# The last batches of a two-layer residual-norm kernel: residual rows added by TensorE, two batches' rows kept in PSUM, openings ahead of closings

## The chip, the cores and the metric

The kernel runs on one core of a Trainium2 chip. The metric is the device time in microseconds of one execution, as the median of several runs. A core has TensorE (PE in the profile: matmuls), VectorE (DVE), ScalarE (ACT), GpSimd (POOL) and SyncE (SP, which here issues the DMAs). SBUF is the working memory. PSUM is where TensorE writes[...].

## The reference

The input x has 128 batches of 128 rows by 512 columns. Layer 0 adds a per-row maximum and normalises. Layer 1 is multi-head attention, a projection, a normalisation inside, a residual sum and a normalisation outside:

```
# layer 0, adj is 128 x 128, b has 128 values
A   = einsum('od,bdn->bon', adj, x);  C = A + b[None, :, None]
x   = layernorm(x + max over the last axis of relu(A[:, :, None, :] + (C - A)[:, :, :, None]))
# layer 1, 8 heads, the mask is adj
q, k, v = split(x @ w_qkv)
o   = softmax(where(adj == 0, -inf, q k^T / sqrt(64))) v
o   = o @ w_proj + b_proj
ln  = (o - mean(o)) * rsqrt(var(o) + 1e-5) * ln_gamma + ln_beta
out = layernorm(x + o + ln)
```

In the kernel's terms, for one batch: r is the row of x after layer 0 (with ln_beta added to it beforehand), o the projected row, and z = (o - mean) * rs * gamma + (o + r), where rs = (var + 1e-5)^-0.5. The output is z normalised again.

## The kernel before

All arithmetic is in float32. Batches are worked on in groups of four (G = 4, NG = 32 groups), and in pairs inside a group. The projections of four batches are a Unit: a 2 x 2 block product by seven half-size products, whose partial sums live in four PSUM banks (b1 to b4) and which `result`, `relay` and `relayed` put together and write to SBUF. The order on every engine is the order in which the program is written (`pin` keeps it): no planner is at work. Where engines depend on one another, semaphores are inserted.

A main loop handles the pairs in a staggered way, and behind it an end section is written out by hand. With L = 127, the end section names the batches L - 7 = 120 to L = 127 one by one. What matters for the change is how the tail, from o to the output, is done for them:

- Batches 116, 117, 122 and 123 go the way of GpSimd: ScalarE normalises o into z (`tail_inner_one`), GpSimd does three residual steps on z (`tail_residual_one`: times gamma, plus o, plus r), ScalarE takes the statistics of z (`scalar_stats`: two accumulating passes per batch, whose unneeded output goes to a PSUM tile "trash"), GpSimd finishes them (`finish_scalar_stats`: names de, me), and ScalarE normalises and stores (`tail_outer_one`).
- Batches 120, 121 and 124 to 127 go the fused way on VectorE: statistics of o (`bn`: BATCH_NORM_STATS2 and BATCH_NORM_AGGREGATE, names st and mv), an **opening** (`fused_open`: z = (o - mean) * gamma, one scalar_tensor_tensor, L624, and r = o + r, a tensor_tensor that shows as L77), a **closing** (`fused_close`: z = z * rs + r, L632), and statistics of z. `finish_stats` has GpSimd work out rs by an addition and a power, and for those columns that ScalarE will normalise with, a shift (VectorE times -1, L267, then GpSimd). The last batch, 127, is normalised by VectorE itself (`tail_outer_vector`, L653).
- Batches 120 and 121 come out of the Unit of group 30 as `os_[30, 0]`, an SBUF tile. Batches 124 to 127 are projected directly: `last_seed` puts the bias in a PSUM bank, and `last_project` adds four products of 128 x 512 to it (names pp). Their rows o are read in PSUM.

The residual rows r of 118 to 121 wait in the SBUF tile "early", those of 122 to 127 in spare room of the tile "wlast", whose other part holds the projection's weights. The tile names zl and z in the profile are the z rows; pss0 and pss1 are the two PSUM banks that the attention scores used.

Three engines' queues matter in the end section. TensorE's order is: projection of 124, attention of 126 and 127, projections of 125, 126 and 127. VectorE's order is that of the openings, closings and statistics as written. GpSimd does residual steps, scales and finishes in the written order. SP issues the stores in the order of the `tail_outer` calls.

Of the kernel before, what the change touches and what calls it, by code (L numbers as in the profile page):

```python
# [9 lines left out]
F32 = mybir.dt.float32  # L10
AF = mybir.ActivationFunctionType
ALU = mybir.AluOpType
# [4 lines left out]
def kernel(  # L17
# [30 lines left out]
    nc = tc.nc  # L48
    B, P, D = x.shape
# [3 lines left out]
    G = 4  # L53
    GT = G * P
    HT = GT // 2
    HE = D // 2
    NG = B // G
# [11 lines left out]
    psum = ctx.enter_context(tc.tile_pool(name="psum", bufs=1, space=bass.MemoryType.PSUM))  # L69

    pin = tc.keep_in_program_order

    def pe(*args, **kwargs):
        pin(nc.tensor.matmul(*args, **kwargs))  # L74

    def tt(eng, dst, a, b, op):
        pin(eng.tensor_tensor(dst, a, b, op))  # L77
# [69 lines left out]
    ident = const.tile([P, P], F32, name="ident")  # L147
# [14 lines left out]
    class Unit:  # L162
# [28 lines left out]
            pin(nc.scalar.copy(self.new_bank(2), self.banks[1]))  # L191

        def relayed(self):
            pin(nc.scalar.copy(self.out[0, 0], self.banks[2]))

        def result(self, half, col):
            bank, k = {(0, 0): (2, 1), (0, 1): (3, 2), (1, 0): (4, 3), (1, 1): (3, 3)}[half, col]
            pin(
                nc.vector.tensor_tensor(  # L199
                    self.out[half, col], self.banks[bank], self.snaps[k], ALU.add  # L200
                )
            )

    def left_sums(name, a11, a12, a21, a22):
        s = [
            sb.tile([P, 2, HT], F32, tag=f"{name[0]}s{k}", name=f"s{k}_{name}") for k in range(1, 5)
        ]
        return dict(zip((1, 2, 3, 4, 5, 6, 7), (a11, a12, s[3], a22, s[0], s[1], s[2]))), (
            (s[0], a21, a22, ALU.add),
            (s[1], s[0], a11, ALU.subtract),  # L210
            (s[2], a11, a21, ALU.subtract),
            (s[3], a12, s[1], ALU.subtract),
        )
# [20 lines left out]
    def tokens_stationary(w):  # L234
        def mm(bank, i, left, first):
            for k in range(2):
                for c in range(2):
                    pe(
                        bank[:, k],
                        lhsT=left[:, c, ts(k, P)],  # L240
                        rhs=w[:, i, c],
                        start=first and k == 0 and c == 0,
                        stop=True,
                        skip_group_check=True,
                    )

        return mm
# [28 lines left out]
    def normalize(dst, src, key):  # L276
        rs, sh = stat_of.pop(key)
        pin(nc.scalar.activation(dst, src, AF.Identity, bias=sh, scale=rs))  # L278
# [104 lines left out]
    pss, prob, psums, pT, pos, oT = {}, {}, {}, {}, {}, {}  # L383
    nmax = {}

    def place(b):
        g, j = divmod(b, G)
        return g, j // 2, j % 2
# [109 lines left out]
    o_lefts, os_ = {}, {}  # L498
# [5 lines left out]

    def o_unit(g):
        for h in range(2):
            tag, bufs = ("x", 2) if (g, h) == (NG - 2, 0) else ("o", 3)
            os_[g, h] = sb.tile([P, 2, D], F32, tag=tag, name=f"o_{g}_{h}", bufs=bufs)
        out = {(h, c): os_[g, h][:, :, ds(c * HE, HE)] for h in range(2) for c in range(2)}
        return Unit(f"o_{g}", o_lefts.get(g), tokens_stationary(wp), out)  # L510


# [19 lines left out]
    def last_project(b, w):  # L532
        g, h, jj = place(b)
        for c in range(KC):
            pe(
                os_[b],
                lhsT=oT[g, h][:, c, ts(jj, P)],
                rhs=w[:, c],
                start=False,
                stop=True,  # L540
                skip_group_check=True,
            )
# [4 lines left out]
    def o_of(b):  # L547
        g, h, jj = place(b)
        return os_[b] if b in os_ else os_[g, h][:, jj]
# [19 lines left out]
    rs_, zp = {}, {}  # L569
# [31 lines left out]
    def z_tile(b):  # L601
        q, j = divmod(b, 2)
        tag, bufs = {58: ("xt", 2), 59: ("xt", 2), 60: ("z", 1), 61: ("qk0", 2)}.get(q, ("xs", 1))
        if tag == "xs":
            zs[b] = sb.tile([P, D], F32, tag=f"xs{b - B + G + 1}", name=f"z_{b}")
            return
        if q not in ends:
            ends[q] = sb.tile([P, 2, D], F32, tag=tag, name=f"zl_{q}", bufs=bufs)
        zs[b] = ends[q][:, j]
# [5 lines left out]
    def tail_residual_one(b, steps=range(3)):  # L615
        for k in steps:
            with_, op = ((ga_bc, ALU.mult), (o_of(b), ALU.add), (rs_[b], ALU.add))[k]
            tt(nc.gpsimd, zs[b], zs[b], with_, op)

    def fused_open(b, mean):  # L620

        z_tile(b)
        pin(
            nc.vector.scalar_tensor_tensor(  # L624
                zs[b], o_of(b), mean, ga_bc, ALU.subtract, ALU.mult
            )
        )
        tt(nc.vector, rs_[b], o_of(b), rs_[b], ALU.add)

    def fused_close(b):  # L630
        z, (rs, _) = zs[b], stat_of.pop(("o", b))
        pin(nc.vector.scalar_tensor_tensor(z, z, rs, rs_[b], ALU.mult, ALU.add))  # L632

    def tail_outer_one(b):
        z = zs.pop(b)
        normalize(z, z, ("z", b))
        pin(nc.sync.dma_start(out=out[b], in_=z))
# [8 lines left out]
    def stats(name, *items, fused=0):  # L646
        stat = columns(name, *items)
        finish_stats(*stat, fused)
        return stat[0]
# [6 lines left out]
    def scalar_stats(*batches):  # L656

        n, name = len(batches), f"{batches[0]}"
        trash = psum.tile([P, D], F32, tag="pss0", name=f"trash_{name}")
        sums, mean, dev = (  # L660
            small.tile([P, NC], F32, tag=f"{t}1", name=f"{t}1_{name}") for t in ("su", "me", "de")
        )
        act = nc.scalar.activation
        for k, b in enumerate(batches):
            pin(act(trash, zs[b], AF.Identity, accum_out=sums[:, k : k + 1]))
        pin(act(mean[:, :n], sums[:, :n], AF.Identity, scale=-1.0 / D))
        for k, b in enumerate(batches):
            pin(
                act(
                    trash, zs[b], AF.Square, bias=mean[:, k : k + 1], accum_out=dev[:, k : k + 1]  # L670
                )
            )
        return batches, mean, dev

    def finish_scalar_stats(stat):
        batches, sh, rs = stat
        n = len(batches)
        pin(nc.gpsimd.tensor_scalar(rs[:, :n], rs[:, :n], 1.0 / D, EPS, ALU.mult, ALU.add))
        tt(nc.gpsimd, rs[:, :n], rs[:, :n], mhalf.to_broadcast([P, n]), ALU.pow)
        tt(nc.gpsimd, sh[:, :n], sh[:, :n], rs[:, :n], ALU.mult)  # L680
        for k, b in enumerate(batches):
            stat_of["z", b] = rs[:, k : k + 1], sh[:, k : k + 1]
# [98 lines left out]
    for p in range(LAST):  # L781
        g, ph = divmod(p, 2)
        a, b = 2 * p, 2 * p + 1
        first = v_unit(0) if p == 0 else qk_unit(g + 1, ph)
        n = p + 4 if p + 4 < B // 2 else None
        f = p + 5 if p + 5 < B // 2 else None
        ta, tb, to = tails(p)
        mv = small.tile([P, NC, 2], F32, tag="mv", name=f"mv_{p}")
# [152 lines left out]
    L = B - 1  # L941
# [10 lines left out]
    mv = small.tile([P, NC, 2], F32, tag="mv", name=f"mv_{LAST}")  # L952
# [101 lines left out]
    wlast, room = last_load()  # L1054
# [101 lines left out]
    mv = stats("last_5", ("o", L - 7), ("o", L - 6), fused=2)  # L1156
    attend_copy(L - 1)
    attend_copy(L)
    last_project(L - 1, wlast)
    last_project(L, wlast)  # L1160
    stat = scalar_stats(L - 11, L - 10)
    tail_residual_one(L - 5, [0])
    fused_open(L - 7, mv[:, 0, 0:1])
    mv1 = stats("last_6", ("o", L - 3), fused=1)
    tail_residual_one(L - 5, [1, 2])
    fused_open(L - 3, mv1[:, 0, 0:1])
    fused_close(L - 7)
    fused_close(L - 3)
    finish_scalar_stats(stat)
    for t in (L - 11, L - 10):  # L1170
        tail_outer_one(t)
    stat5 = scalar_stats(L - 5)
    fused_open(L - 6, mv[:, 1, 0:1])
    mv = stats("last_7", ("o", L - 2), ("z", L - 3), ("z", L - 7), fused=1)
    fused_open(L - 2, mv[:, 0, 0:1])
    fused_close(L - 6)
    fused_close(L - 2)
    tail_residual_one(L - 4)
    for t in (L - 7, L - 3):
        tail_outer_one(t)  # L1180
    mv = stats("last_8", ("o", L - 1), ("z", L - 2), ("z", L - 6), fused=1)
    fused_open(L - 1, mv[:, 0, 0:1])
    fused_close(L - 1)
    finish_scalar_stats(stat5)
    stat4 = scalar_stats(L - 4)
    for t in (L - 6, L - 2, L - 5):
        tail_outer_one(t)
    finish_scalar_stats(stat4)
    mv = stats("last_9", ("o", L), ("z", L - 1), fused=1)
    fused_open(L, mv[:, 0, 0:1])  # L1190
    for t in (L - 4, L - 1):
        tail_outer_one(t)
    fused_close(L)
    mv = stats("last_10", ("z", L), fused=1)
    tail_outer_vector(L, mv[:, 0, 0:1])


# [39 lines left out]
```

## Time and profile before

| | |
|---|---|
| median of 3 runs | 1956.71 us (1956.1 to 1957.49) |
| profiled execution | 1958.7 us, its span 1957.0 us |
| PE, DVE, ACT, POOL busy | 1933.8, 1563.4, 1065.1, 1294.9 us |
| chain that ended last | PE 94%, DVE 2%, POOL 2%, ACT 1%, DMA 1% |
| last matmul ends | 1940.64 us into the span |
| last VectorE instruction | 1953.36 to 1953.91 us |
| last store issued | 1953.93 us |

The difference between the profiled execution and its span lies outside the span, in what surrounds it. In a timeline, each line gives the start in us, the duration in us, the engine, the line of the program, the operation, output <- inputs by tile name, shapes and count, and in brackets the idle time ahead of the instruction with what ended it. In a table of windows each pair is an engine's busy time in the window and, in brackets, its number of instructions, then TensorE's granted clock, the DMA share and the GB/s moved. A chain that ended last is followed back from the last instruction.

### The profile page before, as it was taken

Reading aid. Unit: us, or ns where it says so; the run is one execution under the profiler, and the core shown is the slowest. Engines: PE = TensorE matmul, PEld = TensorE weight load, DVE = VectorE, ACT = ScalarE, POOL = GpSimd, SP = SyncE. Lnnn points to the kernel's source line nnn. Section 1 sums busy time; section 2 is a strip of 40 time slices with the busy share of each in tenths; the row PEclk is TensorE's granted clock in tenths of the full one; section 3 lists DMA queues with packets and bytes.
Section 4 is the critical chain, followed back from the end, with each engine's and each line's share of the span. In section 5 each row is a group of like instructions: output and inputs, shape, how many; then the busy total and the mean of one; then the engine's idle time right before and its main releaser. Section 6 shows DMA issues by size and latency. Waiting matters only on the chain.

```text
span 1957.0 us, 33035 instructions
## 1 busy us (share of the span) xinstructions
PE 1933.8 (99%) x11533; PEld 1637.0 (84%) x11533; DVE 1563.4 (80%) x2516; ACT 1065.1 (54%) x3094; POOL 1294.9 (66%) x820
## 2 busy tenths in 40 slices
PE   8999999999999999999999999999999999999996
PEld 6888888888888888888888888888888888888884
DVE  6767778778788787787787877877878878778787
ACT  3444555545546555555465565554554655555565
POOL 6336666767667676667676676766767766767647
PEclk9999999999999999999999999999999999999998
DMA  6657576575675665766756757667667667576564
GB/s 217 161 136 179 145 194 164 167 207 153 172 193 157 189 173 166 201 154 172 204 153 180 188 157 194 170 165 196 162 171 194 160 186 177 161 201 164 148 216 140
DMA packets 444934, 341.74 MB, mean 175 GB/s; under 512 B 276832, under 2 KB 378336, under 8 KB 444768
## 3 DMA queue, kind: packets, MB, share of 16 engines
q1 hardware_dynamic: 444336, 338.85, 63.8%
q8 instruction: 91, 1.49, 0.3%
q10 hardware_dynamic: 432, 0.79, 0.1%
q14 instruction: 75, 0.61, 0.1%
HBM read 172.82 MB, written 166.72 MB: 174 GB/s over the span
## 4 chain that ended last, share of the span: by engine, by line
PE 94%; DVE 2%; POOL 2%; ACT 1%; DMA 1%; issue 0%; SPq 0%; POOLq 0%; ACTq 0%; DVEq 0%
PE b_qk L74 39%; PE b_v L74 19%; PE b_o L74 18%; PE pss L74 6%; PE po L74 6%; PE pa L74 5%; POOL zl L77 1%; DVE st_mv_last L255 0%; ACT s L424 0%; POOL s_o L77 0%; DMA x<-in_x_dram 0%; DMA pT<-hop 0%; POOL rs_mv_last L77 0%; DMA hop<-pu 0%; DVE amax L291 0%
## 5 line engine op out<-in xcount | busy, mean ns | idle before, releaser
L74 PE MATMUL b_qk<-s_x,wqk 128*128 128x256 f32 x2048 | 473.6, 379 | 1.0 <-DVE qk L199 0.8
L74 PEld LDWEIGHTS b_qk<-s_x,wqk 128*128 128x128 f32 x2048 | 388.8, 190 | 55.4 <-DVE qk L199 1.5
L424 ACT ACTIVATE s<-s,nmax 128x128 f32<-128x128 f32 x1024 | 396.2, 392 | 5.3 <-DVE nmax L417 5.3
L74 PE MATMUL b_qk<-x1T,wqk 128*128 128x256 f32 x1536 | 360.1, 384 | 0.1
L74 PEld LDWEIGHTS b_qk<-x1T,wqk 128*128 128x128 f32 x1536 | 287.8, 191 | 45.5 <-issue 1.0
L77 POOL TENSOR_TENSOR z<-z,ga_bc 128x1024 f32<-128x1024 f32 x58 | 164.6, 2838 | 167.1 <-ACT z L278 167.1
L269 POOL TENSOR_SCALAR rs_mv<-mv 128x6 f32<-128x6 f32 (+2 forms) x61 | 14.7, 241 | 386.3 <-DVE mv L256 386.3
L77 DVE TENSOR_TENSOR s<-s,rec 128x1024 f32<-128x1024 f32 x128 | 252.8, 1975 | 4.4
L186 ACT COPY u_qk<-b_qk 128x512 f32<-128x512 f32 x192 | 112.5, 586 | 243.3 <-PE b_qk L74 242.4
L74 PE MATMUL b_v<-wv,s_x 128*128 128x256 f32 x1024 | 237.1, 379 | 0.0
L74 PE MATMUL b_o<-wp,s_o 128*128 128x256 f32 x992 | 229.6, 379 | 0.2 <-ACT u_o L186 0.2
L74 PEld LDWEIGHTS b_v<-wv,s_x 128*128 128x128 f32 x1024 | 194.4, 190 | 26.9 <-ACT u_v L186 0.4
L405 DVE SCALAR_TENSOR_TENSOR s<-pss,mask 128x512 f32<-128x512 f32 x256 | 164.2, 683 | 61.8 <-PE pss L74 61.7
L74 PEld LDWEIGHTS b_o<-wp,s_o 128*128 128x128 f32 x992 | 188.2, 190 | 26.4 <-issue 0.8
L199 DVE TENSOR_TENSOR qk<-b_qk,u_qk 128x512 f32<-128x512 f32 x256 | 168.0, 675 | 48.9 <-PE b_qk L74 44.9
L77 POOL TENSOR_TENSOR x<-x,be_bc 128x1024 f32<-128x1024 f32 x64 | 181.3, 2834 | 33.6 <-DVE rec L435 27.9
L424 ACT ACTIVATION_READ_ACCUMULATOR s<-s,nmax 128x1 f32 x1024 | 195.1, 191 | 0.0
L199 DVE TENSOR_TENSOR v<-b_v,u_v 128x512 f32<-128x512 f32 x127 | 86.2, 680 | 133.7 <-PE po L74 128.9
L186 ACT COPY u_o<-b_o 128x512 f32<-128x512 f32 x91 | 53.3, 586 | 239.0 <-PE b_o L74 239.0
L186 ACT COPY u_v<-b_v 128x512 f32<-128x512 f32 x95 | 55.7, 586 | 233.2 <-PE b_v L74 233.2
L74 PE MATMUL b_v<-wv,x1T 128*128 128x256 f32 x768 | 176.5, 379 | 0.0
L74 PEld LDWEIGHTS b_v<-wv,x1T 128*128 128x128 f32 x768 | 145.8, 190 | 32.3 <-issue 13.9
(128 smaller groups left out, 3398.7 us busy)
## 6 DMA issues: line engine op xcount, KB each, us to landing
hop<-pu SPq DMA_DIRECT2D x128, 512.0 KB, 3.7
pT<-hop SPq DMA_DIRECT2D x512, 128.0 KB, 3.7
spill<-x SPq DMA_DIRECT2D x64, 512.0 KB, 4.8
x<-in_x_dram SPq DMA_DIRECT2D x62, 512.0 KB, 4.5
xhop<-xt SPq DMA_DIRECT2D x248, 128.0 KB, 2.3
x1T<-xhop SPq DMA_DIRECT2D x248, 128.0 KB, 3.9
xr<-spill SPq DMA_DIRECT2D x59, 512.0 KB, 3.6
out_dram<-xr SPq DMA_DIRECT2D x58, 512.0 KB, 4.1
```

The lines of the kernel that those rows point to most:

```text
L74: pin(nc.tensor.matmul(*args, **kwargs))
L77: pin(eng.tensor_tensor(dst, a, b, op))
L186: pin(nc.scalar.copy(t, self.banks[1]))
L199: nc.vector.tensor_tensor(self.out[half, col], self.banks[bank], self.snaps[k], ALU.add)
L269: pin(nc.gpsimd.tensor_scalar(rs[:, :n], mv[:, :n, 1], EPS, None, ALU.add))
L405: nc.vector.scalar_tensor_tensor(s[:, par], pss[b][par], SCALE, mask.unsqueeze(1).to_broadcast([P, NP, P]), ALU.mult, ALU.add,)
L424: nc.scalar.activation(prob[b][:, i], prob[b][:, i], AF.Exp, bias=nmax[b][:, i : i + 1], accum_out=psums[b][:, i : i + 1],)
```

## The change

Rows 120 and 121 of o are no longer assembled in SBUF: `o_unit` puts them in the PSUM banks pss0 and pss1, one bank for each batch, so `relayed` and `result` write them in two halves (`places`). The other two batches of the group stay in SBUF. The "trash" tile of `scalar_stats` moves from bank pss0 to bank po.

For batches 124 to 127, `fused_open` leaves out VectorE's r = o + r. In its place `add_rows` has TensorE multiply r by the identity and accumulate it onto o in the PSUM bank, after the opening has read o there; the closing then reads that bank as its row.

The order is written anew: the openings stand ahead of closings of other batches, the projections of 126 and 127 behind the row adds of 124 and 125, the third residual step of 122 and of 123 later in the program, the finishing of the statistics of 122 and 123 elsewhere, and the stores accordingly. There is one more call of statistics, since z of 126 gets its own.

```
--- before.py
+++ after.py
@@ -191,15 +191,21 @@
             pin(nc.scalar.copy(self.new_bank(2), self.banks[1]))
 
         def relayed(self):
-            pin(nc.scalar.copy(self.out[0, 0], self.banks[2]))
+            for dst, src in self.places(0, 0, self.banks[2]):
+                pin(nc.scalar.copy(dst, src))
+
+        def places(self, half, col, bank):
+
+            out = self.out[half, col]
+            return [(d, bank[:, k]) for k, d in enumerate(out)] if type(out) is list else [(out, bank)]
 
         def result(self, half, col):
             bank, k = {(0, 0): (2, 1), (0, 1): (3, 2), (1, 0): (4, 3), (1, 1): (3, 3)}[half, col]
-            pin(
-                nc.vector.tensor_tensor(
-                    self.out[half, col], self.banks[bank], self.snaps[k], ALU.add
-                )
-            )
+            adds = zip(
+                self.places(half, col, self.banks[bank]), self.places(half, col, self.snaps[k])
+            )
+            for (dst, a), (_, b) in adds:
+                tt(nc.vector, dst, a, b, ALU.add)
 
     def left_sums(name, a11, a12, a21, a22):
         s = [
@@ -504,9 +510,22 @@
 
     def o_unit(g):
         for h in range(2):
-            tag, bufs = ("x", 2) if (g, h) == (NG - 2, 0) else ("o", 3)
+            if (g, h) == (NG - 2, 0):
+                continue
+            tag, bufs = "o", 3
             os_[g, h] = sb.tile([P, 2, D], F32, tag=tag, name=f"o_{g}_{h}", bufs=bufs)
-        out = {(h, c): os_[g, h][:, :, ds(c * HE, HE)] for h in range(2) for c in range(2)}
+        out = {
+            (h, c): os_[g, h][:, :, ds(c * HE, HE)]
+            for h in range(2)
+            for c in range(2)
+            if (g, h) in os_
+        }
+        if g == NG - 2:
+
+            for j in range(2):
+                os_[g * G + j] = psum.tile([P, D], F32, tag=f"pss{j}", name=f"o_{g * G + j}")
+            for c in range(2):
+                out[0, c] = [os_[g * G + j][:, ds(c * HE, HE)] for j in range(2)]
         return Unit(f"o_{g}", o_lefts.get(g), tokens_stationary(wp), out)
 
 
@@ -617,7 +636,7 @@
             with_, op = ((ga_bc, ALU.mult), (o_of(b), ALU.add), (rs_[b], ALU.add))[k]
             tt(nc.gpsimd, zs[b], zs[b], with_, op)
 
-    def fused_open(b, mean):
+    def fused_open(b, mean, rows=True):
 
         z_tile(b)
         pin(
@@ -625,11 +644,17 @@
                 zs[b], o_of(b), mean, ga_bc, ALU.subtract, ALU.mult
             )
         )
-        tt(nc.vector, rs_[b], o_of(b), rs_[b], ALU.add)
+        if rows:
+            tt(nc.vector, rs_[b], o_of(b), rs_[b], ALU.add)
 
     def fused_close(b):
         z, (rs, _) = zs[b], stat_of.pop(("o", b))
         pin(nc.vector.scalar_tensor_tensor(z, z, rs, rs_[b], ALU.mult, ALU.add))
+
+    def add_rows(b):
+
+        pe(os_[b], lhsT=ident, rhs=rs_[b], start=False, stop=True, skip_group_check=True)
+        rs_[b] = os_[b]
 
     def tail_outer_one(b):
         z = zs.pop(b)
@@ -656,7 +681,7 @@
     def scalar_stats(*batches):
 
         n, name = len(batches), f"{batches[0]}"
-        trash = psum.tile([P, D], F32, tag="pss0", name=f"trash_{name}")
+        trash = psum.tile([P, D], F32, tag="po", name=f"trash_{name}", bufs=1)
         sums, mean, dev = (
             small.tile([P, NC], F32, tag=f"{t}1", name=f"{t}1_{name}") for t in ("su", "me", "de")
         )
@@ -1156,42 +1181,49 @@
     mv = stats("last_5", ("o", L - 7), ("o", L - 6), fused=2)
     attend_copy(L - 1)
     attend_copy(L)
-    last_project(L - 1, wlast)
-    last_project(L, wlast)
     stat = scalar_stats(L - 11, L - 10)
     tail_residual_one(L - 5, [0])
     fused_open(L - 7, mv[:, 0, 0:1])
     mv1 = stats("last_6", ("o", L - 3), fused=1)
-    tail_residual_one(L - 5, [1, 2])
-    fused_open(L - 3, mv1[:, 0, 0:1])
+    tail_residual_one(L - 5, [1])
+    fused_open(L - 3, mv1[:, 0, 0:1], rows=False)
+    add_rows(L - 3)
+    last_project(L - 1, wlast)
+    fused_open(L - 6, mv[:, 1, 0:1])
     fused_close(L - 7)
-    fused_close(L - 3)
+    fused_close(L - 6)
+    tail_residual_one(L - 5, [2])
     finish_scalar_stats(stat)
     for t in (L - 11, L - 10):
         tail_outer_one(t)
     stat5 = scalar_stats(L - 5)
-    fused_open(L - 6, mv[:, 1, 0:1])
-    mv = stats("last_7", ("o", L - 2), ("z", L - 3), ("z", L - 7), fused=1)
-    fused_open(L - 2, mv[:, 0, 0:1])
-    fused_close(L - 6)
+    mv = stats("last_7", ("o", L - 2), ("z", L - 7), fused=1)
+    fused_open(L - 2, mv[:, 0, 0:1], rows=False)
+    add_rows(L - 2)
+    last_project(L, wlast)
+    fused_close(L - 3)
+    tail_residual_one(L - 4, [0, 1])
+    tail_outer_one(L - 7)
+    mv = stats("last_8", ("o", L - 1), ("z", L - 6), ("z", L - 3), fused=1)
+    fused_open(L - 1, mv[:, 0, 0:1], rows=False)
+    add_rows(L - 1)
     fused_close(L - 2)
-    tail_residual_one(L - 4)
-    for t in (L - 7, L - 3):
+    finish_scalar_stats(stat5)
+    tail_residual_one(L - 4, [2])
+    for t in (L - 3, L - 6, L - 5):
         tail_outer_one(t)
-    mv = stats("last_8", ("o", L - 1), ("z", L - 2), ("z", L - 6), fused=1)
-    fused_open(L - 1, mv[:, 0, 0:1])
+    stat4 = scalar_stats(L - 4)
+    mv = stats("last_9", ("o", L), ("z", L - 2), fused=1)
+    fused_open(L, mv[:, 0, 0:1], rows=False)
+    add_rows(L)
     fused_close(L - 1)
-    finish_scalar_stats(stat5)
-    stat4 = scalar_stats(L - 4)
-    for t in (L - 6, L - 2, L - 5):
+    tail_outer_one(L - 2)
+    stats("last_10", ("z", L - 1))
+    finish_scalar_stats(stat4)
+    fused_close(L)
+    for t in (L - 1, L - 4):
         tail_outer_one(t)
-    finish_scalar_stats(stat4)
-    mv = stats("last_9", ("o", L), ("z", L - 1), fused=1)
-    fused_open(L, mv[:, 0, 0:1])
-    for t in (L - 4, L - 1):
-        tail_outer_one(t)
-    fused_close(L)
-    mv = stats("last_10", ("z", L), fused=1)
+    mv = stats("last_11", ("z", L), fused=1)
     tail_outer_vector(L, mv[:, 0, 0:1])
```

## The prediction, made before the result was known

> **What bounds the kernel now.** The first view is the head of the page. TensorE is busy for 99% of the span and carries 94% of the chain that ended last, so for most of the time nothing but TensorE counts. The change does not touch that part. It touches the closing stretch, so the second view is the table of windows over the last 31 us.
>
> ```profile
> core 0: us, PE busy (x) PEld busy (x) DVE busy (x) ACT busy (x) POOL busy (x), PEclk, DMA share, GB/s
> ...
> 1930.00:1934.00 4.00, 4.00 (x12) 1.82 (x10) 3.86 (x6) 3.87 (x10) 3.84 (x6) 1.00 0.09 35
> 1934.00:1938.00 4.00, 4.00 (x11) 1.81 (x10) 3.93 (x8) 0.90 (x3) 3.06 (x4) 1.00 0.00 0
> 1938.00:1942.00 4.00, 2.63 (x7) 0.85 (x5) 3.97 (x9) 3.48 (x9) 2.88 (x4) 1.00 0.35 131
> 1942.00:1946.00 4.00, 0.00 (x0) 0.00 (x0) 3.27 (x9) 1.10 (x3) 3.76 (x5) 0.79 0.36 133
> 1946.00:1950.00 4.00, 0.00 (x0) 0.00 (x0) 3.31 (x8) 3.75 (x9) 3.26 (x10) 0.50 0.31 114
> 1950.00:1954.00 4.00, 0.00 (x0) 0.00 (x0) 2.69 (x5) 1.15 (x2) 1.58 (x4) 0.50 0.57 216
> ```
>
> TensorE's last matmul ends at 1940.64. From 1928 to 1942 VectorE is full (3.86 to 3.97 of 4 us), and after 1942 VectorE and GpSimd take turns. The third view, VectorE's timeline, shows what fills it. The lines kept here are the slow ones and a normal one of each kind.
>
> ```profile
> 1932.43 1.76 DVE L632 SCALAR_TENSOR_TENSOR z<-z,rs_mv_last,wlast 128x512 f32<-128x512 f32 x1
> 1934.11 1.75 DVE L624 SCALAR_TENSOR_TENSOR zl<-o,mv_last,ga_bc 128x512 f32<-128x512 f32 x1
> ...
> 1938.91 0.75 DVE L624 SCALAR_TENSOR_TENSOR z<-pp,mv_last,ga_bc 128x512 f32<-128x512 f32 x1
> 1939.58 0.68 DVE L77 TENSOR_TENSOR wlast<-pp,wlast 128x512 f32<-128x512 f32 x1
> 1940.17 0.74 DVE L632 SCALAR_TENSOR_TENSOR zl<-zl,rs_mv_last,early 128x512 f32<-128x512 f32 x1
> ...
> 1946.59 0.78 DVE L632 SCALAR_TENSOR_TENSOR z<-z,rs_mv_last,wlast 128x512 f32<-128x512 f32 x1 [1.21 <-POOL rs_mv_last L77]
> ...
> 1953.36 0.55 DVE L653 TENSOR_SCALAR z<-z,mv_last,rs_mv_last 128x512 f32<-128x512 f32 x1 [1.00 <-POOL rs_mv_last L77]
> ```
>
> A closing (L632) and an opening (L624) that take 0.74 and 0.75 us elsewhere take 1.76 and 1.75 us here: 2.0 us are lost. GpSimd's timeline for the same moments shows the other half.
>
> ```profile
> 1932.22 1.42 POOL L77 TENSOR_TENSOR zl<-zl,o 128x512 f32<-128x512 f32 x1
> 1933.72 1.60 POOL L77 TENSOR_TENSOR zl<-zl,wlast 128x512 f32<-128x512 f32 x1
> ...
> 1940.93 1.78 POOL L77 TENSOR_TENSOR zl<-zl,ga_bc 128x512 f32<-128x512 f32 x1
> 1942.78 1.26 POOL L77 TENSOR_TENSOR zl<-zl,o 128x512 f32<-128x512 f32 x1
> ```
>
> A GpSimd residual step takes 1.26 us alone and 1.42 to 1.78 us beside a closing or an SBUF opening. Both engines pay. The wait of 1.21 us at 1946.59 is GpSimd delivering batch 126's scale late, because the three residual steps of batch 123 (1940.93 to 1945.39) were ahead of it.
>
> **What the Trainium skill says.** "SBUF — State Buffer", section "Who interferes with whom": a VectorE instruction with two SBUF inputs contends with a GpSimd instruction that reads SBUF, one of them blocks fully until the other ends, and a VectorE instruction with at most one SBUF input doesn't contend. The trace agrees: the 1.75 us opening read o and ga_bc, both in SBUF, while the opening at 1944.03, which read pp in PSUM, took 0.75 us beside GpSimd's residual step of 1942.78 and 1944.12 (1.26 and 1.27 us). "PSUM — Partial Sum Buffer", section "Engine vs sequencer instructions": matmuls start and complete in program order. So an identity add that waits holds up every projection behind it; in the trace the projections follow one another without a gap from 1930.07.
>
> **The change, part by part.** I replay the stretch from 1928 with start-to-start steps of this trace. VectorE: opening 0.67, row add 0.60, closing 0.67 (0.81 when its own statistics come next, 1950.64 to 1951.45), one row's statistics 0.80, shift 0.12. GpSimd: residual step 1.34, or 1.23 with a small operation behind it; scale: add 0.31, power 0.63, 0.79 or 0.96 for 1, 2 or 3 columns, shift 0.28 (0.15 ahead of a residual step); finishing ScalarE statistics 0.27+0.63+0.28.
>
> *Rows 120 and 121 in PSUM.* The relay on ScalarE and one result on VectorE become two halves each. VectorE's halves: "VectorE: DVE Perf Modes" prices a tensor_tensor at (N+151)/0.96 ns, so 0.42 us for 256 columns; the trace has 0.68 for 512 (0.69 by that price). With overlap the pair costs 0.06 us more. No row of before has VectorE writing PSUM: I bound it by -0.1 and +0.3 and take +0.06, on the path, since the statistics of 121 and 120 follow at once. ScalarE's pair costs some 0.2 us (two of about 0.37 from 0.59 for 512) and lies in the 2.13 us for which ScalarE waits until 1916.79; without that cover it would delay the normalising of 116. The gain: the openings of 120 and 121 have one SBUF input left. The SBUF buffer that falls away, and the statistics' scratch moved to bank "po" behind ScalarE's own copy out of it, cost nothing: that is one engine's order.
>
> *Row adds to TensorE.* Four VectorE adds go: 4 x 0.60 = 2.4 us. TensorE gets four identity products; from 24 records in 10.57 us, two records are 0.88 us each (at half clock 1.76). TensorE's queue is then: project 125 to 1933.59, add 124 to 1934.47, project 126 to 1937.99, add 125 to 1938.87, project 127 to 1942.39, add 126 to 1943.27, add 127 when its opening is done. New waits: add 124 waits for its opening (over at 1931.3), hidden by project 125; add 125 for its opening (1937.4), hidden by project 126. Behind them stand projections 126 and 127, for which VectorE's statistics wait. Row 127 is asked for at 1942.9, so 0.5 us is spare. Closings 124 to 127 now read their row in PSUM: between 0.67 and 0.8 us, taken as 0.67, and without contention.
>
> *The new order.* Opening 120 starts at 1928.27, add 120 at 1928.95, statistics 124 at 1929.56, opening 124 at 1930.56, opening 121 at 1931.23, add 121 at 1931.91. Closing 120 comes up at 1932.51. GpSimd, no longer blocked by the openings, ends batch 122's second residual step at 1932.75, so the closing loses 0.23 us and ends at 1933.3 (VectorE ends 0.55 us after it gets in, as at 1934.19). GpSimd's third step takes the next turn to 1934.43, and closing 121 ends at 1934.97. Statistics of 120 and 125 start at 1934.89; opening 125 at 1936.61, where before had 1938.91 at this place. That is 2.3 us: 0.6 for one row add, 0.8 for one row's statistics moved later, and 0.9 less blocking. From there VectorE has no large instruction with two SBUF tensors: closing 124 1937.28, three statistics to 1940.58, opening 126 1940.62, closing 125 1941.29, statistics of 125 and 127 to 1943.78, opening 127 1943.82, closing 126 1944.49, its statistics to 1946.18, closing 127 1946.22, its statistics to 1947.94.
>
> *GpSimd becomes the chain.* Scale of 125 from 1936.62, residual steps 1 and 2 of batch 123 1937.87 to 1940.44, scale of 126 from 1940.63, finish 122 to 1943.24, third step to 1944.47, scale of 127 to 1945.85, scale of 126's second normalising (waits for VectorE) 1946.22 to 1947.44, finish 123 to 1948.62, last scale 0.88 to 1949.50. The last VectorE instruction starts at 1949.52 instead of 1953.36: **3.84 us earlier**. The 1.21 us wait goes; VectorE's last wait stays, 1.6 us in place of 1.0, because batch 123's finish is ahead of it. ScalarE has 123's statistics ready at 1946.5, before GpSimd asks at 1947.44.
>
> *Queues.* Every store is still issued, by SP in the order in which ScalarE normalises; the store of 123 leaves at about 1949.8, that of 127 at about 1950.1, so two transfers overlap where before the last was alone (landing 2.0 to 2.1 us): 0 to 0.3 us, not counted.
>
> The profiled execution took 1958.7 us, its span 1957.0, the median is 1956.71. Less 3.8: 1954.9, 1953.2 and **1952.9**.
>
> **Rivals.** *GpSimd does not bind.* If its small operations run closer together, only VectorE's chain counts: last scale at 1947.99, plus 0.88, so 4.5 us saved, and up to 0.9 more if the two closings never meet a residual step. 1951.3 to 1952.2, centre 1951.9. For it: GpSimd's durations in the profile are rough. Against it: its steps were taken from start to start.
>
> *The contention stays.* The two closings 120 and 121 still read two SBUF tensors beside batch 122's residual steps. If they lose 2.0 us as before, and GpSimd with them, 0.9 to 1.3 us of the gain goes, and a late ScalarE statistic can take as much again: 1.3 to 2.9 us saved, some 1954.6. For it: two closings now stand in a row, just where GpSimd is busy.
>
> *TensorE's queue turns on it (slower).* Add 125 stands ahead of projection 127. If it waits for more than its opening, say the work of VectorE behind it, projection 127 slides. Spare are 0.6 us (1937.36 to 1937.99) and 0.5 us at row 127, so a wait of 1.1 us is free, 5.0 us eats the whole gain, and from 8.9 us the kernel is slower by over 0.2%: 1961. Against it: VectorE reaches opening 125 with nothing but its own work ahead, and TensorE has no idle time in this stretch now.
>
> **How the numbers follow.** 0.2% is 3.9 us, about what a measurement of this kernel can tell from no change. My case (0.60) ends at 1952.9, its own range 1952.2 to 1953.6 lies on both sides of the line at 1952.8: 0.30 faster, 0.30 within. GpSimd not binding (0.20) is faster. Contention (0.14) is within. TensorE's queue (0.06) is slower. Sums: 0.50, 0.44, 0.06. The range 1951.2 to 1955.2 takes in the first three cases but for their ends.
>
> **What would show it.** Right: no row add on wlast from VectorE, openings at 0.75 us throughout, opening 125 near 1936.6, TensorE without a gap up to about 1943.3, VectorE's last wait on GpSimd at 1.3 to 1.9 us with GpSimd busy from 1936 to 1949. Wrong: an idle time of TensorE above 1 us ahead of a pp matmul, closings 120 and 121 at 1.7 us, or a last VectorE instruction later than 1951.

## The result and the profile after

| | before | changed |
|---|---|---|
| median | 1956.49 us (13 runs) | 1952.91 us (13 runs) |
| profiled execution and span | 1958.7 and 1957.0 us | 1953.87 and 1951.6 us |
| closing stretch | 31.82 us | 28.08 us |

The ratio is 0.9982 with a 95% interval of 0.9974 to 0.9989: 3.6 us (0.18%) faster. The interval leaves out 1, and the value is just short of the 0.2% at which the prediction drew its line.

The **closing stretch** is the yardstick of what follows. It runs from the start of VectorE's pair of results for rows 122 and 123 (`o<-b_o,u_o`, two together, 1921.54 before and 1919.96 after) to the start of VectorE's last instruction (1953.36 and 1948.04). It is shorter by 3.74 us. The two spans differ by 5.4 us because the profiled execution of the changed kernel was already 1.58 us ahead where the stretch begins: the same product starts at 301.72 us before and at 300.15 after, and 1.1 us of that is there within the first 15 us, where TensorE waits for the first input loads. In the ten profiled executions of this document the stretch begins anywhere from 1918.73 to 1921.54. So a time of the changed trace is compared with one of before, or with one of the prediction, after adding 1.58. No kernel was profiled twice, so the scatter of the stretch itself is not measured; its first 6.8 us, up to opening 120, agree within 0.03 us in the seven kernels that have rows 120 and 121 in PSUM.

First the table of windows of the changed kernel (busy us of PE, PEld, DVE, ACT, POOL, in brackets the instructions).

```profile
1938.00:1942.00 4.00, 4.00 (x10) 1.52 (x8) 3.86 (x10) 1.88 (x3) 3.48 (x8) 1.00 0.19 70
1942.00:1946.00 4.00, 1.23 (x3) 0.30 (x2) 3.76 (x10) 3.41 (x9) 3.19 (x8) 1.00 0.53 197
1946.00:1950.00 4.00, 0.00 (x0) 0.00 (x0) 1.02 (x3) 1.51 (x2) 1.68 (x5) 0.59 0.66 248
```

TensorE's last matmul ends at 1944.19; with 1.58 added that is 5.1 us later than before, of which the four adds are 3.7, a wait for opening 127 0.95 and a later start of projection 125 0.5. VectorE is full up to 1946 (3.76 of 4 us, where before had 3.27 and 3.31 in its last two full windows), and after that little is left. The next view is VectorE's timeline: start, duration, operation, and in brackets the idle time ahead.

```profile
1929.01 0.75 DVE L643 SCALAR_TENSOR_TENSOR z<-pp,mv_last,ga_bc 128x512 f32<-128x512 f32 x1
1929.67 0.74 DVE L643 SCALAR_TENSOR_TENSOR zl<-o,mv_last,ga_bc 128x512 f32<-128x512 f32 x1
1930.33 0.68 DVE L77 TENSOR_TENSOR early<-o,early 128x512 f32<-128x512 f32 x1
1930.93 2.50 DVE L652 SCALAR_TENSOR_TENSOR zl<-zl,rs_mv_last,early 128x512 f32<-128x512 f32 x2
...
1935.09 0.75 DVE L643 SCALAR_TENSOR_TENSOR z<-pp,mv_last,ga_bc 128x512 f32<-128x512 f32 x1
1935.76 0.74 DVE L652 SCALAR_TENSOR_TENSOR z<-z,rs_mv_last,pp 128x512 f32<-128x512 f32 x1
...
1948.04 0.55 DVE L678 TENSOR_SCALAR z<-z,mv_last,rs_mv_last 128x512 f32<-128x512 f32 x1 [1.53 <-POOL rs_mv_last L77]
```

Every opening now takes 0.74 or 0.75 us, opening 121 (1929.67) among them, which took 1.75. No row add on wlast is left. Closing 124 (1935.76) reads its row in pp. Only closings 120 and 121 still lose time: 2.50 us for two that need 1.4 alone. The 1.21 us wait for batch 126's scale is gone, and the last wait has grown from 1.00 to 1.53 us.

TensorE's timeline shows the new queue, and GpSimd's what stands ahead of the last scale.

```profile
1928.96 3.70 PE L74 MATMUL pp<-wlast,oT 128*128 128x512 f32 x8
1932.50 1.02 PE L74 MATMUL pp<-wlast,ident 128*128 128x512 f32 x2
1933.36 3.60 PE L74 MATMUL pp<-wlast,oT 128*128 128x512 f32 x8
1936.79 1.02 PE L74 MATMUL pp<-wlast,ident 128*128 128x512 f32 x2
1937.65 3.60 PE L74 MATMUL pp<-wlast,oT 128*128 128x512 f32 x8
1941.09 1.02 PE L74 MATMUL pp<-wlast,ident 128*128 128x512 f32 x2
1943.06 1.13 PE L74 MATMUL pp<-wlast,ident 128*128 128x512 f32 x2 [0.95 <-DVE z L643]
```

```profile
1931.28 1.60 POOL L77 TENSOR_TENSOR zl<-zl,wlast 128x512 f32<-128x512 f32 x1
...
1944.69 0.23 POOL L275 TENSOR_SCALAR rs_mv_last<-mv_last 128x1 f32<-128x1 f32 x1 [0.32 <-DVE mv_last L262]
...
1946.85 0.19 POOL L77 TENSOR_TENSOR me<-me,de 128x1 f32<-128x1 f32 x1
1947.13 0.23 POOL L275 TENSOR_SCALAR rs_mv_last<-mv_last 128x1 f32<-128x1 f32 x1
```

An identity add costs 0.86 us from start to start, and TensorE runs from 1928.96 to the end of add 126 without a wait. GpSimd starts the last scale (1947.13) 0.6 us after VectorE has the numbers for it (1946.51), straight behind batch 123's finish.

### The profile page after: what moved, and what is told of

The parts are those of the page before. It is cut to its first block, busy times and chain, and to the rows that moved or that the text cites. A ratio compares the mean times of both kernels' runs of the same rounds, so it can differ in the third digit from the quotient of the medians.

```text
span 1951.6 us, 33053 instructions
## 1 busy us (share of the span) xinstructions
PE 1937.1 (99%) x11541; PEld 1638.4 (84%) x11541; DVE 1560.6 (80%) x2514; ACT 1065.2 (55%) x3095; POOL 1293.7 (66%) x823
## 3 DMA queue, kind: packets, MB, share of 16 engines
q8 instruction: 91, 1.49, 0.3%
## 4 chain that ended last, share of the span: by engine, by line
PE 95%; DVE 2%; POOL 1%; ACT 1%; DMA 0%; issue 0%; SPq 0%; POOLq 0%; ACTq 0%; DVEq 0%
PE b_qk L74 40%; PE b_v L74 19%; PE b_o L74 18%; PE pss L74 6%; PE po L74 6%; PE pa L74 5%; DVE st_mv_last L261 0%; POOL zl L77 0%; DMA x<-in_x_dram 0%; ACT s L430 0%; POOL s_o L77 0%; DVE amax L297 0%; DVE mv_last L262 0%; DVE o L77 0%; DVE pu L451 0%
```

## The experiments

My theory: the parts work together. TensorE's adds shorten VectorE's queue, but only in an order in which VectorE asks for a row after TensorE can have added it, and the rows in PSUM and the order reduce what VectorE and GpSimd take from one another. The rival: each part counts by itself. A second rival was TensorE's queue. The stretches below come from one profiled execution each, the ratios (against before, with their intervals) from repeated runs.

### Rows 120 and 121 in PSUM, alone

```
 # kernel before, with places(), o_unit() and "trash" of the change
-tag="pss0", name=f"trash_{name}"
+tag="po", name=f"trash_{name}", bufs=1
```

> One part alone: rows 120 and 121 in PSUM and the scratch in bank po, with VectorE's row adds and the order of before. The measure is the closing stretch, from the start of VectorE's pair of results for rows 122 and 123 (o<-b_o,u_o x2) to the start of VectorE's last instruction: 31.82 us before, 28.08 us after the change. Theory A (the parts work together): opening 121 falls from 1.75 to 0.75 us, but GpSimd, which the openings no longer hold up, is earlier and the two closings that follow now meet its residual steps, so most of the 1.0 us is lost again: stretch 31.6, between 30.8 and 31.9. Rival B (each part counts by itself): the 0.9 to 1.0 us of blocking goes: 30.8 to 30.9.

Measured: stretch 31.60 us, 0.22 less than before; ratio 0.9999 (0.9991 to 1.0007). VectorE's timeline of this kernel:

```profile
1929.24 1.47 DVE L651 SCALAR_TENSOR_TENSOR zl<-zl,rs_mv_last,early 128x512 f32<-128x512 f32 x1
1930.64 1.75 DVE L651 SCALAR_TENSOR_TENSOR z<-z,rs_mv_last,wlast 128x512 f32<-128x512 f32 x1
1932.32 0.74 DVE L643 SCALAR_TENSOR_TENSOR zl<-o,mv_last,ga_bc 128x512 f32<-128x512 f32 x1
```

Opening 121 (the last line) is down to 0.74 us from 1.75, but closing 120, which stands ahead of it, is up to 1.47 from 0.74, and closing 124 stays at 1.75. GpSimd, which opening 120 and its row add no longer block, has come forward and now meets both closings. Of the gain of 1.0 us, 0.73 is lost again there and 0.07 on the half-size results, as theory A said.

### The changed kernel without those PSUM rows

```
 # changed kernel, with relayed(), result() and o_unit() of before
-os_[g * G + j] = psum.tile([P, D], F32, tag=f"pss{j}", ...)
+os_[g, h] = sb.tile([P, 2, D], F32, tag="x", ...)
```

> The changed kernel with rows 120 and 121 back in SBUF; TensorE's row adds and the new order stay. Closing stretch 28.08 us in the changed kernel. Theory A: openings 120 and 121 again have two SBUF inputs and hold GpSimd up, whose residual steps then fall on the closings; 0.5 to 1.2 us are lost: 28.9, between 28.4 and 29.3. Rival B: the SBUF openings now meet no residual step and nothing is lost: 28.0 to 28.2.

Measured: stretch 28.67 us, 0.59 more than the changed kernel; ratio 0.9985 (0.9977 to 0.9992), which can't be told from the 0.9982 of the changed kernel. Theory A's number came out, but not by its path. GpSimd's timeline shows how an opening with its row in SBUF, and the row add behind it, hold it up:

```profile
1926.04 0.66 POOL L269 TENSOR_SCALAR rs_mv_last<-mv_last 128x2 f32<-128x2 f32 x1
1926.78 1.01 POOL L77 TENSOR_TENSOR rs_mv_last<-rs_mv_last,mhalf 128x2 f32<-128x2 f32 x1
```

The same two small operations take 0.22 and 0.72 us in the changed kernel. VectorE's openings hardly suffer (0.77 us each), and closings 120 and 121 don't either: the pair takes 2.42 us, against 2.50 in the changed kernel, and opening 125 starts 15.02 us into the stretch, against 15.13. GpSimd suffers. It ends residual step 2 of batch 122 1.6 us later in the stretch, and it is still 0.7 us late at step 2 of batch 123. VectorE's two-column shift, which takes 0.14 us in the changed kernel, now ends only when that step does:

```profile
1937.67 1.26 POOL L77 TENSOR_TENSOR zl<-zl,o 128x512 f32<-128x512 f32 x1
```

```profile
1938.04 0.92 DVE L267 TENSOR_SCALAR sh_mv_last<-mv_last 128x2 f32<-128x2 f32 x1
```

From start to start the shift costs 0.72 us more; less the 0.11 us by which VectorE was ahead, that is the whole loss. So in these traces the PSUM rows are worth 0.2 us in the old order and 0.6 in the new one, and in the new one they earn it by keeping one small instruction clear of GpSimd, not by shorter openings or closings.

### The changed kernel with VectorE's row adds

```
-    fused_open(L - 3, mv1[:, 0, 0:1], rows=False)
-    add_rows(L - 3)
+    fused_open(L - 3, mv1[:, 0, 0:1])        # and so for L - 2, L - 1, L
```

> The changed kernel with the row adds of 124 to 127 back on VectorE; rows 120 and 121 in PSUM and the new order stay, and nothing of TensorE's projections waits any more. Closing stretch 28.08 us in the changed kernel. Theory A: four adds of 0.60 us come back into VectorE's queue, one of them where it waits for GpSimd's residual step anyway, and closings 124 to 127 again have two SBUF inputs: 30.4, between 29.9 and 31.2. Rival B: GpSimd's own chain from row 125's scale to the end hides part of the adds: 29.0 to 29.6.

Measured: stretch 31.67 us, 3.59 more than the changed kernel and only 0.15 less than before; ratio 0.9999 (0.9991 to 1.0007). Both theories gave too little, mine by 1.3 us. From start to start against the changed kernel, VectorE is late by 0.31 us at opening 125, 2.02 at the statistics of z of 124, 2.62 at those of 125, 3.21 at those of 126, 3.59 at the end. Three adds account for 1.8 of it, and the 0.31 is what reaches opening 125 of the fourth. What I had priced too low is in these two lines, VectorE's closing 124 and GpSimd's power for 126:

```profile
1936.92 1.84 DVE L652 SCALAR_TENSOR_TENSOR z<-z,rs_mv_last,wlast 128x512 f32<-128x512 f32 x1
```

```profile
1948.47 0.96 POOL L77 TENSOR_TENSOR rs_mv_last<-rs_mv_last,mhalf 128x1 f32<-128x1 f32 x1
```

Closing 124 with its row in SBUF meets a residual step of batch 123 and loses 1.1 us; the power takes 0.96 us in place of 0.58 beside closing 127. Moving the sum into PSUM not only takes 0.60 us from VectorE for each row, it also takes the closing out of the contention. And the new order with the PSUM rows, but without TensorE's adds, is worth next to nothing.

### TensorE's adds alone, in the old order

```
+    add_rows(L - 3)
+    last_project(L - 1, wlast)      # kernel before; likewise add 125 and projection 127, adds 126 and 127
```

> Another part alone: the kernel before with the row adds of 124 to 127 on TensorE (projections 126 and 127 behind adds 124 and 125, since they share a queue), rows 120 and 121 in SBUF, VectorE's and GpSimd's order as before. Closing stretch 31.82 us before, 28.08 after the change. Theory A: in the old order closing 124 stands right behind its opening, and TensorE can add row 124 only when projection 125 is done, so VectorE waits there some 2.5 us; projection 127 starts only when row 125 is open, and row 126's scale comes as late as before: 31.7, between 31.0 and 32.3, nothing won. Rival B (four VectorE adds count 0.60 us each whatever the order): 29.4.

Measured: stretch 33.16 us, 1.34 more than before; ratio 1.0012 (1.0006 to 1.0019), so 0.12% slower. The place of the cost was right, the size was not. VectorE's and TensorE's timelines:

```profile
1932.86 0.75 DVE L633 SCALAR_TENSOR_TENSOR z<-z,rs_mv_last,pp 128x512 f32<-128x512 f32 x1 [2.68 <-PE pp L74]
...
1939.36 0.75 DVE L633 SCALAR_TENSOR_TENSOR z<-z,rs_mv_last,pp 128x512 f32<-128x512 f32 x1 [0.63 <-PE pp L74]
...
1944.72 0.75 DVE L633 SCALAR_TENSOR_TENSOR z<-z,rs_mv_last,pp 128x512 f32<-128x512 f32 x1 [1.29 <-PE pp L74]
...
1950.24 0.75 DVE L633 SCALAR_TENSOR_TENSOR z<-z,rs_mv_last,pp 128x512 f32<-128x512 f32 x1 [2.23 <-PE pp L74]
```

```profile
1938.13 1.12 PE L74 MATMUL pp<-wlast,ident 128*128 128x512 f32 x2 [1.94 <-DVE z L624]
1939.09 3.60 PE L74 MATMUL pp<-wlast,oT 128*128 128x512 f32 x8
1943.49 1.12 PE L74 MATMUL pp<-wlast,ident 128*128 128x512 f32 x2 [0.81 <-DVE z L624]
1948.06 2.07 PE L74 MATMUL pp<-wlast,ident 128*128 128x512 f32 x2 [3.44 <-DVE z L624]
```

Every closing of a row that TensorE adds stands at most one closing behind its own opening here, so VectorE waits for TensorE four times, 6.8 us in all. The expectation had only the first of them in full. About 1 us of the last wait is the add itself, which takes 2.07 us instead of 1.02. The waits cost only 1.34 net, because four adds (2.4 us), the blocking of closing 124 and opening 121 (2.0) and the wait of 1.21 us for batch 126's scale are gone. Taking four adds from VectorE is worth nothing where it then waits for them. The repeated runs put the loss at 2.3 us (0.12% of 1956.4), 1 us more than the trace; that difference stays open.

### Projections ahead of the adds

```
     attend_copy(L)
+    last_project(L - 1, wlast)
+    last_project(L, wlast)          # changed kernel; taken out behind adds 124 and 125
```

> The changed kernel with the projections of 126 and 127 where they were before, ahead of all row adds in TensorE's queue. Closing stretch 28.08 us in the changed kernel, 31.82 before. Theory A: add 124 now comes after projection 127, some 4.6 us after the point at which VectorE asks for closing 124; VectorE waits there once and nothing else changes: 32.7, between 32.0 and 33.2, slower than before by 0.2 to 1.4 us. Rival B (GpSimd's chain sets the end and hides part of the wait): 30 to 31.

Measured: stretch 32.32 us, 4.24 more than the changed kernel; ratio 1.0004 (0.9996 to 1.0012), not told apart from before. Closing 124 waits once, for add 124 behind two projections:

```profile
1938.80 0.75 DVE L652 SCALAR_TENSOR_TENSOR z<-z,rs_mv_last,pp 128x512 f32<-128x512 f32 x1 [4.18 <-PE pp L74]
```

The wait of 4.18 us returns whole at the end, as theory A said. A second one, of 0.38 us at closing 127, does not: VectorE's last wait on GpSimd is shorter by about as much (1.10 us, 1.53 in the changed kernel). So TensorE's place in the order is as much a part of the gain as VectorE's.

### A longer queue ahead of row 127

```
+    for _ in range(4):
+        pe(os_[L], lhsT=zeros[:, :P], rhs=rs_[L], start=False, stop=True, skip_group_check=True)
     last_project(L, wlast)
```

> The changed kernel with four products by a matrix of zeros (they add nothing) ahead of the projection of row 127: 4 x 0.86 = 3.4 us more on TensorE's queue. Closing stretch 28.08 us in the changed kernel. The prediction on record says that 1.1 us of such a delay is free: then 30.4. The trace of the changed kernel says that row 127's last product ends only some 0.2 us ahead of VectorE's statistics of it (1941.34): then 31.3, with VectorE idle by some 3.2 us ahead of those statistics. If GpSimd's chain alone set the end, the delay would cost less than 2: below 30.

Measured: stretch 30.91 us, 2.83 more than the changed kernel; ratio 0.9997 (0.9989 to 1.0006). VectorE:

```profile
1942.91 0.70 DVE L261 BATCH_NORM_STATS2 st_mv_last<-pp 128x6 f32<-128x512 f32 x1 [2.76 <-PE pp L74]
```

Statistics of row 127 start 2.80 us later relative to the start of the stretch, so 0.6 of the 3.4 us were free and the rest went straight to the end. The expectation misread the record: its 1.1 us were 0.6 ahead of add 125 and 0.5 at row 127, and products put behind add 125 can use only the second. The rival of TensorE's queue was a real danger with a margin of about half a microsecond.

### One finish for 122 and 123

```
-    tail_residual_one(L - 4, [0, 1])
+    tail_residual_one(L - 4)
     tail_outer_one(L - 7)
+    stat5 = scalar_stats(L - 5, L - 4)
...
     fused_close(L - 1)
+    finish_scalar_stats(stat5)       # in place of a finish for each
```

> The changed kernel with less on GpSimd's chain: the third residual step of 123 right behind the first two, ScalarE's statistics of 122 and 123 as one pair, finished by one call (1.34 us in place of two of 1.18) between the scales of 127 and of 126's second normalising, so that nothing stands ahead of the last scale. Closing stretch 28.08 us in the changed kernel. Theory A: VectorE's queue up to the statistics of 127 is unchanged, and its last wait on GpSimd falls from 1.53 to about 0.95 us, as it was before the change: 27.5, between 27.3 and 27.8. Rival B (GpSimd is only behind because VectorE is, and the longer residual block of 123 makes the scale of 126 or 127 late): 28.1 to 29.

Measured: stretch 27.53 us, 0.55 less than the changed kernel, and VectorE's last instruction:

```profile
1947.33 0.55 DVE L678 TENSOR_SCALAR z<-z,mv_last,rs_mv_last 128x512 f32<-128x512 f32 x1 [1.01 <-POOL rs_mv_last L77]
```

The last wait is back at 1.01 us. Up to the statistics of 127 VectorE is where it was (25.6 us into the stretch in both), so in the trace batch 123's finish ahead of the last scale did cost half a microsecond. Against before the ratio is 0.9981 (0.9974 to 0.9989), with a median of 1952.84 us: over the repeated runs this can't be told from the changed kernel.

### The same, with closings 120 and 121 kept clear of a residual step

```
-    tail_residual_one(L - 5, [2])
     finish_scalar_stats(stat)
+    tail_residual_one(L - 5, [2])
```

> The kernel with one finish for 122 and 123, and besides the third residual step of 122 behind the finish of 116 and 117, so that closings 120 and 121 meet one residual step in place of two and lose some 0.2 us in place of 1.1. Theory A: VectorE is earlier by about 1 us up to the statistics of row 127, which it can't start before TensorE has projected that row (0.05 us of spare in the trace of the changed kernel, 0.6 us in that of the four products): the stretch is shorter than with one finish by 0.1 to 0.5 us, 27.2, between 26.9 and 27.5. Rival B (VectorE alone sets the pace): 1 us shorter, 26.5.

Measured: stretch 26.96 us; ratio 0.9981 (0.9974 to 0.9989), median 1953.05 us. VectorE:

```profile
1931.15 1.49 DVE L652 SCALAR_TENSOR_TENSOR zl<-zl,rs_mv_last,early 128x512 f32<-128x512 f32 x2
...
1940.94 0.70 DVE L261 BATCH_NORM_STATS2 st_mv_last<-pp 128x6 f32<-128x512 f32 x1 [0.33 <-PE pp L74]
```

The two closings take 1.49 us in place of 2.50, and a wait for TensorE at row 127 takes a third of the microsecond that was won: 0.57 us reaches the last VectorE instruction. It does not reach the end of the span. From there to the end it takes 4.24 us (1947.16 to 1951.4) where one finish takes 3.57 (1947.33 to 1950.9). SyncE's timeline shows why it starts late:

```profile
1947.74 0.33 SPq L662 DMA_DIRECT2D out_dram<-z  x1
1948.17 0.40 SPq L679 DMA_DIRECT2D out_dram<-z  x1
```

The last store is issued at 1948.17, 0.46 us after VectorE has finished (1947.71), right behind the store of 126, for which ScalarE was only now done. How much of the rest is the two transfers' overlap was not measured by itself.

## Why the prediction was right

| step | predicted | measured, plus 1.58 |
|---|---|---|
| opening 125 | 1936.61 | 1936.67 |
| opening 126 | 1940.62 | 1940.65 |
| opening 127 | 1943.82 | 1943.84 |
| closing 127 | 1946.22 | 1946.40 |
| last scale on GpSimd | 1948.62 | 1948.71 |
| last VectorE instruction | 1949.52 | 1949.62 |
| stretch shorter by | 3.84 us | 3.74 us |

**The replay** held, point by point. Replaying the queues from start-to-start steps of the profile before, with the contention written in as turns, gave each point within 0.2 us. That the median of 1952.91 lies on the forecast to 0.01 us is luck: the 3.8 us were taken from the 1956.71 of three runs, where 13 runs give 1956.49 and a fall of 3.58. What the forecast said of where the gain comes from held less well, as the next three points show.

**The row adds.** The term of 2.4 us was right for what leaves VectorE. The prediction also said that closings 124 to 127 would be free of contention, but gave that no figure of its own; with VectorE's adds put back it is 1.1 us at closing 124 and 0.4 at the end, and the adds are worth 3.6 us in this order.

**Blocking.** The forecast had 0.9 us less of it by opening 125, with closing 121 over at 1934.97. It was over at 1935.01 (1933.43 and 1.58). But the forecast put this gain down to openings with one SBUF input, and that was wrong: with rows 120 and 121 back in SBUF and the new order kept, VectorE reaches opening 125 no later (15.02 us into the stretch, 15.13 in the changed kernel). It is the order that brings it. What the PSUM rows bring was at the two-column shift, a term that the forecast took as 0.12 us everywhere.

**The shift of 128 x 2** cost nothing by luck. The forecast held that a VectorE instruction with at most one SBUF input doesn't contend. This shift reads one SBUF tile, and without the PSUM rows it was held up until a GpSimd step ended. In the changed kernel it starts (1938.95) 0.06 us before the same step ends (1939.01), and so loses almost nothing. ("SBUF — State Buffer", section "Who interferes with whom" in the Trainium skill, makes an exception for VectorE's 2-port modes, which the forecast's wording left out; whether this shift ran in one, no run here shows.)

```profile
1938.95 0.14 DVE L273 TENSOR_SCALAR sh_mv_last<-mv_last 128x2 f32<-128x2 f32 x1
```

**GpSimd as the chain** was put too strongly. In the changed kernel GpSimd waits for VectorE at two scales, 0.58 us at 1935.14 and 0.32 at 1944.69. The chain of waits runs through VectorE up to 1944.6 and only then through GpSimd, over the last 3.4 us; taking GpSimd's finish out of the way there gave 0.55 us. The case that carried 0.20 of the chance, GpSimd not binding, asked for 4.5 us or more: no kernel came to that without moving GpSimd's work.

**Half-size results.** Predicted at 0.06 us more; the pair took 0.75 us against 0.68, right.

**TensorE's queue** did not turn: no wait ahead of a projection in the pp sequence. The spare at row 127 was priced at 0.5 us, and 0.6 was measured with the four products. In the profiled execution it was nearer 0.05: the attention product of 127 waited 0.35 us, which no profile of an experiment shows, and the projections behind it start 0.58 us later in the stretch than with the four products. That VectorE did not wait there was close.

```profile
1927.94 1.09 PE L74 MATMUL po<-pT,v 128*64 128x128 f32 x16 [0.35 <-ACT zl L284]
```

**Stores**: an overlap of 0 to 0.3 us, not counted, was harmless: 3.01 us from the end of VectorE to the end of the span, 3.09 before. With the stores closer together the store queue is not harmless: in the last experiment the last store is issued 0.46 us after VectorE's end.

## What to carry to other kernels

Where two engines hold each other up and a third hands results back, price a change by replaying the queues from start to start, not by adding up the durations that go: here the same row adds were worth 3.6 us in one order and cost 1.3 us in the other. An accumulation moved to TensorE helps twice, since the instruction that reads its sum from PSUM no longer takes a second SBUF input, but every consumer must stand behind other work, or it waits. Near a balance of three engines, look for the next wait before taking one away: half a microsecond further on it was TensorE, and then the store queue.

## What the runs showed of the hardware that I had not expected

An identity add takes 1.02 us in a busy queue, but took 2.07 us in the old order (after 3.44 us without work) and 2.08 with the projections first. The length of the wait just ahead does not decide it, as TensorE's timeline of the latter shows:

```profile
1942.93 1.13 PE L74 MATMUL pp<-wlast,ident 128*128 128x512 f32 x2 [3.37 <-DVE z L643]
1946.11 2.08 PE L74 MATMUL pp<-wlast,ident 128*128 128x512 f32 x2 [2.06 <-DVE z L643]
```

What goes with it is the granted clock: 1.00 from 1942 to 1944, at the add that took 1.13 us, and 0.50 from 1946 to 1948, at the one that took 2.08; in the old order it was 0.50 from 1948 to 1950. When the clock falls is not worked out here. A row add left to the end, when TensorE has little to do, can cost double; in the changed kernel it did not (1.13 us).

Contention reaches GpSimd's smallest operations: a power over one column took 0.96 us beside a closing with two SBUF inputs, and 0.58 in the changed kernel, beside one with its row in PSUM. It reaches VectorE's shift of 128 x 2 as well, which reads one SBUF tile: 0.92 us behind a residual step without the PSUM rows (and 1.24 at 1924.60 of the kernel before), 0.14 at the same place in the changed kernel.
